# Transposes of the identity in the planned stands of TensorE, in a block of attention between two expert layers

## Chip, core and metric

The kernel runs on one core of a Trainium2 chip. Time is the device time of one execution in microseconds (us); lower is better. The five engines are TensorE (PE, its weight loads shown apart as PEld), VectorE (DVE), ScalarE (ACT), GpSimd (POOL) and SyncE (SP); each works through its own queue of instructions in order.

## What is computed

The input is x, 2 sequences of 4,096 tokens of width 256, in float32. The reference, cut to its steps:

```python
x = x + 0.5 * ffn(layernorm(x), gate_w, w1, w2, w3)
x = x + attn(layernorm(x), Wq, Wk, Wv, Wb, conv_q_w, conv_k_w, conv_v_w, rms_w, Wo)
x = x + 0.5 * ffn(layernorm(x), gate_w, w1, w2, w3)
```

`ffn` sends each token to 2 of 8 experts by a softmax over `x @ gate_w`; an expert is `(silu(xs @ w1) * (xs @ w3)) @ w2` with 128 hidden columns. `attn` has 4 heads of 64 columns: projections, a causal convolution over 4 tokens and silu for q, k and v, then a recurrence over chunks of tokens with a 64 x 64 state per head (a triangular system per chunk, `mid = U - W S`, an output, and `S = S + mid.T @ K`), a root-mean-square norm and `Wo`.

## The kernel before

**Tiles and stages.** Work comes in units of 4 x 128 tokens (256 of each sequence). For an expert layer, units are taken in groups. `prepare` (line 739) normalises, routes and scatters the rows of a group into DRAM by expert (`slots`, POOL's indirect DMAs, line 712). `experts` (line 793) takes 256 slots at a time: two weight tiles `we` by DMA, the rows `xi` by DMA, four transposes into the PSUM tile `pxi`, a copy to `xiT`, eight products into `p13` (the profile's `p_a`, `p_b`; a product of float32 shows as two rows), silu and product into `hs`, two products into `py`, a copy to `yo` and a DMA to `made`. `combine` (line 852) gathers rows back (line 730) and adds.

Attention is done in steps of two units. `project` (line 884) makes q, k, v (`ptx`, `pj`, `pb`). `gram` and `substitute` (line 999) solve 32 x 32 triangles on VectorE through DRAM. For each chunk of 128 tokens `inverse` (line 1031) loads the results (`XT`, `X`) and builds the inverse from small products (`pp`, `px`, `pq`, `pz`), and `advance` (line 1081) runs the recurrence (`pa`, `pk`, `pv`, `pks`, `pmid`, `po`, `pds`); `finish` norms, transposes (`pto`) and projects (`pyo`).

**Names.** `_a` and `_b` in a tile's name stand for the first and the second expert layer (and `_a` for tiles of attention's units). PSUM tiles come from one pool with two buffers for each of four tags, `tr`, `fa`, `at` and `y`; each buffer is one bank.

**What sets the order.** Nearly no instruction is issued where it is written. `plan` (class `Plan`, line 43) records each call with its reads, writes and a cost; `order` (line 183) then plays the whole program once, before it is issued, as a greedy list schedule over the five engines, and `issue` (line 360) gives the operations out in that order. PE, DVE, ACT and SP then follow it as it stands. The model in `order`:

- `cost` (line 111) gives the time of a VectorE, ScalarE or GpSimd operation by its columns; `dma` (line 105) that of a transfer, which lands 1.4 us after its issue (2.0 us for an indirect one) and its own time.
- `stream` (line 144) gives the time and the weight of a product; a transpose of 128 columns takes 0.84 x 128 + 2 ns, 55 more behind a stand.
- TensorE's clock is modelled in windows of 3,413 ns: after a window that streamed fewer than 1,450 columns, everything takes 1.9 times as long in the next (line 335).
- A PSUM tile is given a buffer when the operation that first writes it has all its predecessors planned (`offer`, line 273); the operation starts no sooner than the buffer came free (line 285).

`t` is the planned start of the operation that is taken next, and `free["tensor"]` the planned end of TensorE's last one. Where `t` is later, the plan sees TensorE stand.

Of the kernel before, what the change touches and what calls it, by code (L numbers as in the profile page):

```python
# [42 lines left out]
class Plan:  # L43
# [11 lines left out]

    def __init__(self, nc):
        self.nc = nc
        self.ops, self.tiles = [], {}
        for name in self.ENGINES:
            setattr(self, name, Plan.Engine(self, name))  # L60

# [14 lines left out]
    class Pool:  # L76
# [5 lines left out]
        def tile(self, shape, dtype, tag=None, name=None, bufs=None):  # L82
            kw = {} if bufs is None else {"bufs": bufs}
            t = self.pool.tile(shape, dtype, tag=tag, name=name, **kw)
            self.plan.tiles[t.tensor.name] = (id(self), tag, bufs or self.bufs)
            return t

    @staticmethod
# [94 lines left out]
    def order(self):  # L183
        ops, N = self.ops, len(self.ops)
# [67 lines left out]
        own, rank, count, slots = [[] for _ in range(N)], {}, {}, {}  # L252
        for m, (pool, tag, bufs) in self.tiles.items():
            if m in users:
                key = (pool, tag)
# [4 lines left out]
                    own[k].append(m)  # L260
        left = {m: len(users[m]) for m in rank}
        ended = {m: 0.0 for m in rank}
        given, taken, waiting = set(), dict.fromkeys(slots, 0), {}
        need = [len(b) for b in before]
        for k in range(N):
            for j in before[k]:
# [1 line left out]
        at = [0.0] * N  # L268
        coming = {e: [] for e in self.ENGINES}
        ready = {e: [] for e in self.ENGINES}  # L270
        free = dict.fromkeys(self.ENGINES, 0.0)

        def offer(k):
            new = sorted((m for m in own[k] if m not in given), key=lambda m: rank[m])
            want = {}
            for m in new:
                key = self.tiles[m][:2]
                n = want.get(key, 0)
                if rank[m] != taken[key] + n or len(slots[key]) <= n:
                    waiting.setdefault(key, []).append(k)  # L280
                    return
                want[key] = n + 1
            for m in new:
                key = self.tiles[m][:2]
                at[k] = max(at[k], heapq.heappop(slots[key]) + self.HEED[ops[k][0]])
                taken[key] += 1
                given.add(m)
            heapq.heappush(coming[ops[k][0]], (at[k], k))
            for key in want:
                for j in waiting.pop(key, ()):  # L290
                    offer(j)

        for k in range(N):
            if need[k] == 0:
                offer(k)
# [3 lines left out]

        W, window, streamed, pace = 3413.0, 0, 0.0, 1.9  # L300
        last = (True, 128, 128, 128, 0)
        result = []
        while len(result) < N:
            best = None
            for e in self.ENGINES:
                while coming[e] and coming[e][0][0] <= free[e]:
                    k = heapq.heappop(coming[e])[1]
                    heapq.heappush(ready[e], k)
                if ready[e]:
                    t = free[e]  # L310
                elif coming[e]:
                    t = coming[e][0][0]
                else:
                    continue
                if best is None or t < best[0]:
                    best = (t, e)
            t, e = best
            while coming[e] and coming[e][0][0] <= t:
                heapq.heappush(ready[e], heapq.heappop(coming[e])[1])
            k = heapq.heappop(ready[e])  # L320
            cost = ops[k][4]
            if cost[0] == "dma":
                _, size, soft, extra = cost
                lane = turn[soft] % self.QUEUES
                t = max(t + extra, lanes[soft][lane] + 50)
                end = moved = max(t + (2000 if soft else 1400), moved) + size
                lanes[soft][lane] = end
                turn[soft] += 1
                free[e] = t + (1278 if soft else 430)
            else:  # L330
                if e == "tensor":
                    end = t
                    for product in cost:
                        while end >= (window + 1) * W:
                            pace = 1.0 if streamed >= 1450 else 1.9
                            window, streamed = window + 1, 0.0
                        c, m = self.stream(product, last, end > free[e] + 6)
                        streamed, last = streamed + m, product
                        end = free[e] = end + c * pace
                    end += 165  # L340
                else:
                    end, free[e] = t + cost[1], t + cost[0]
            result.append(k)
            for j in behind[k]:
                need[j] -= 1
                same = ops[j][0] == e == "tensor"
                at[j] = max(at[j], free[e] if same else end + self.HEED[ops[j][0]])
                if need[j] == 0:
                    offer(j)
            for m in own[k]:  # L350
                left[m] -= 1
                ended[m] = max(ended[m], end)
                if left[m] == 0:
                    key = self.tiles[m][:2]
                    heapq.heappush(slots[key], ended[m])
                    for j in waiting.pop(key, ()):
                        offer(j)
        return result, max(free.values())

    def issue(self):  # L360
        order, _ = self.order()
        for k in order:
            self.ops[k][1]()


@with_exitstack
def kernel(
# [22 lines left out]
    E, _, FH = w1.shape  # L390
# [28 lines left out]
    plan = Plan(nc)  # L419
# [17 lines left out]
    ident = const.tile([P, P], F32, name="ident")  # L437
# [42 lines left out]


    nc = plan


    WROW = 2 * KC * FH + DM
# [30 lines left out]
    slots = [dram.tile([NTL * P, DM], F32, name=f"slots_{i}") for i in range(2)]  # L516
# [775 lines left out]
    for n in range(-1, NS):  # L1292
        (i0, f0), (i1, f1) = PLAN[n + 1], PLAN[n + 2]
        c0, c1 = cost_of(i0, f0), cost_of(i1, f1)
        for part in range(2):
# [11 lines left out]
            if n + 1 < NS:  # L1307
                c = PROJECT_COST + 2 * GRAM_COST + part * SUB_COST
# [56 lines left out]
```

## Time and profile before

| | |
|---|---|
| median of 10 executions | 2186.46 us (2176.47 to 2193.56) |
| profiled execution, time / span | 2173.45 us / 2171.6 us |
| mean granted clock of TensorE | 0.859 |
| PE busy | 1625.7 us, 12,324 rows |
| DVE, POOL, ACT busy | 1198.8, 732.4, 728.2 us |
| moved by DMA | 418.01 MB, a mean of 192 GB/s |

The span runs from the first to the last instruction. Busy time is the time in which an engine has an instruction in work. The profile cuts the span into 40 slices and gives the busy share of each in tenths; `PEclk` is the clock that TensorE was granted, in tenths of full speed. A line of waits names who waited for whom, the sum in us, how many times, and the longest. In a timeline, a line holds the start, the duration, engine, line (72 is the helper that issues all planned operations), operation, output and inputs, and how many; the bracket at its end is the idle time before it. In a table of stretches a line holds the stretch, its length, the busy time and count of each engine, the granted clock, the DMA engines' busy share and GB/s.

### The profile page before, as it was taken

What the parts mean: (1) busy time and instruction counts of PE and PEld (TensorE: products, weight loads), DVE (VectorE), ACT (ScalarE), POOL (GpSimd) and SP (SyncE); (2) the same over time, 40 slices, a digit from 0 to 9 for tenths busy, and PEclk for the clock granted to TensorE, in tenths of its full rate; (3) what the DMA queues carried; (4) which work ended last, traced back from release to release, by engine and by line L of the source; (5) the groups of instructions that cost most, each with busy time, mean ns of one, the idle gap of its engine ahead of it and who ended that gap; (6) DMA issues with size and microseconds to landing.
All of it is one profiled execution on the core that took longest, in us unless ns stands there. A gap on an engine that the chain in (4) does not pass through costs nothing. (4 is left out here: it accounts for less than half of the span.)

```text
span 2171.6 us, 36805 instructions
## 1 busy us (share of the span) xinstructions
PE 1625.7 (75%) x12324; PEld 1267.6 (58%) x12324; DVE 1198.8 (55%) x3737; ACT 728.2 (34%) x1402; POOL 732.4 (34%) x833
## 2 busy tenths in 40 slices
PE   2645965689849996995988599669989858797653
PEld 1434643467637775774766377557757646686442
DVE  4423733786467666466556846656684447344422
ACT  1232443233534432343432324523332432231220
POOL 3144145411664311114455111653110462024342
PEclk7778987989869996997979789869988879698777
DMA  9778776745577552546668234765453768368875
GB/s 370 240 260 276 241 227 209 236 117 159 160 227 213 162 164 62 145 121 191 208 189 260 83 98 119 249 198 158 119 152 105 234 216 265 109 206 278 266 259 152
DMA packets 369406, 418.01 MB, mean 192 GB/s; under 512 B 124480, under 2 KB 304704, under 8 KB 369216
## 3 DMA queue, kind: packets, MB, share of 16 engines
q1 hardware_dynamic: 343280, 345.35, 51.9%
q0 software_dynamic: 24576, 67.14, 9.3%
q10 hardware_dynamic: 1360, 3.16, 0.4%
q8 instruction: 98, 1.61, 0.3%
q14 instruction: 92, 0.75, 0.1%
HBM read 288.51 MB, written 130.15 MB: 193 GB/s over the span
## 5 line engine op out<-in xcount | busy, mean ns | idle before, releaser
L72 PE MATMUL p_b<-xiT_b,we_b 128*128 128x128 f32 x1344 | 210.6, 298 | 67.2 <-ACT hs_b L72 41.3
L72 PEld LDWEIGHTS p_b<-xiT_b,we_b 128*128 128x128 f32 x1344 | 182.5, 204 | 106.7 <-ACT hs_b L72 56.6
L72 PE MATMUL p_a<-xiT_a,we_a 128*128 128x128 f32 x1280 | 195.9, 292 | 49.3 <-ACT hs_a L72 37.4
L72 DVE SCALAR_TENSOR_TENSOR cv_a<-pre_a,cw_sb,cv_a 128x512 f32<-128x512 f32 x288 | 213.3, 746 | 27.6 <-ACT cv_a L72 24.2
L72 PEld LDWEIGHTS p_a<-xiT_a,we_a 128*128 128x128 f32 x1280 | 169.2, 198 | 86.0 <-ACT hs_a L72 52.5
L72 PE MATMUL pj_a<-xT_a,wp_sb 128*128 128x512 f32 x384 | 195.8, 621 | 10.7 <-ACT cv_a L72 9.2
L712 POOL DMA_INDIRECT slots<-row_b,sli_b x128 | 129.6, 1013 | 154.8 <-ACT row_b L72 71.4
L712 POOL DMA_INDIRECT slots<-row_a,sli_a x128 | 129.5, 1012 | 144.7 <-ACT row_a L72 62.5
L730 POOL DMA_INDIRECT got_b<-made,sli_b x128 | 126.7, 989 | 143.9 <-DMA made<-yo_b 38.5
L730 POOL DMA_INDIRECT got_a<-made,sli_a x128 | 127.6, 997 | 109.2 <-DVE x_a_2c L72 19.8
L72 POOL TENSOR_TENSOR rr<-ms,mhalf 128x8 f32<-128x8 f32 x32 | 53.7, 1679 | 270.8 <-DVE ms L72 236.8
L72 PE MATMUL pxi_a<-ident,xi_a 128*128 128x128 f32 x320 | 53.7, 289 | 72.4 <-DMA xi_a<-slots 72.0
L72 POOL COPY carry<-pre_a 128x6 f32<-128x6 f32 x96 | 27.9, 291 | 229.0 <-ACT pre_a L72 228.6
L72 PE MATMUL py_a<-we_a,hs_a 128*128 128x256 f32 x320 | 93.0, 408 | 9.2 <-DVE hs_a L72 6.3
L72 DVE TENSOR_TENSOR hs_b<-p_b,hs_b 128x256 f32<-128x256 f32 x84 | 35.6, 423 | 115.1 <-PE p_b L72 110.4
L72 PE MATMUL py_b<-we_b,hs_b 128*128 128x256 f32 x336 | 96.2, 405 | 3.7 <-DVE hs_b L72 1.5
L72 PEld LDWEIGHTS pj_a<-xT_a,wp_sb 128*128 128x128 f32 x384 | 67.9, 198 | 52.3 <-issue 32.8
L72 ACT COPY pre_a<-pj_a 128x512 f32<-128x512 f32 x96 | 56.2, 585 | 121.3 <-PE pj_a L72 109.2
L72 DVE TENSOR_TENSOR hs_a<-p_a,hs_a 128x256 f32<-128x256 f32 x80 | 33.9, 423 | 111.6 <-PE p_a L72 106.4
L72 PEld LDWEIGHTS pxi_a<-ident,xi_a 128*128 128x128 f32 x320 | 41.0, 149 | 91.8 <-DMA xi_a<-slots 68.2
L72 PE MATMUL pxi_b<-ident,xi_b 128*128 128x128 f32 x336 | 55.9, 293 | 46.3 <-DMA xi_b<-slots 46.3
L72 PE MATMUL pyo<-wo_sb,oT 128*128 128x256 f32 x256 | 71.9, 426 | 20.0 <-ACT oT L72 20.0
(240 smaller groups left out, 3658.3 us busy)
## 6 DMA issues: line engine op xcount, KB each, us to landing
we_b<-wcat SPq DMA_DIRECT2D x168, 384.0 KB
we_a<-wcat SPq DMA_DIRECT2D x160, 384.0 KB
xi_b<-slots SPq DMA_DIRECT2D x84, 256.0 KB
made<-yo_b SPq DMA_DIRECT2D x84, 256.0 KB
xi_a<-slots SPq DMA_DIRECT2D x80, 256.0 KB
made<-yo_a SPq DMA_DIRECT2D x80, 256.0 KB
slots<-XT SPq DMA_DIRECT2D x9, 1024.0 KB
x_a<-in_L_attn_x_dram SPq DMA_DIRECT2D x32, 256.0 KB
```

Of the source, the lines that this page charges most:

```text
L72: self.plan.add(self.name, lambda: real(*args, **kw), ins, outs, cost)
L712: ins = tc.nc.gpsimd.indirect_dma_start(out=dst, out_offset=bass.IndirectOffsetOnAxis(ap=slot, axis=0), in_=row, in_offset=None,)
L730: return tc.nc.gpsimd.indirect_dma_start(out=got, out_offset=None, in_=src, in_offset=bass.IndirectOffsetOnAxis(ap=slot, axis=0),)
```

## The change

Each PSUM tile with 128 partitions and at least 128 columns is kept by name with a view of its first 128 columns (`banks`). When `offer` gives such a tile its buffer, it also enters the tile in `blank` with the time from which the buffer is free; when an operation that writes the tile is planned, the tile leaves `blank`.

When TensorE's next operation is taken, the planner looks at the time between the end of its last operation and the start `t`. As long as some tile is blank, it takes the one that has been free longest and puts a transpose of the identity (`filler`: 128 x 128) into it, as long as that transpose ends before `t - 100 - 0.1 * gap` ns by the plan. The tile's name goes into the order, and `issue` gives out the transpose there. The model counts it as a product like any other, for TensorE's time and for the clock. The operation that the tile is meant for writes over it later. The diff:

```diff
--- before.py
+++ after.py
@@ -55,7 +55,7 @@
 
     def __init__(self, nc):
         self.nc = nc
-        self.ops, self.tiles = [], {}
+        self.ops, self.tiles, self.banks = [], {}, {}
         for name in self.ENGINES:
             setattr(self, name, Plan.Engine(self, name))
 
@@ -83,6 +83,11 @@
             kw = {} if bufs is None else {"bufs": bufs}
             t = self.pool.tile(shape, dtype, tag=tag, name=name, **kw)
             self.plan.tiles[t.tensor.name] = (id(self), tag, bufs or self.bufs)
+            if t.space == bass.MemoryType.PSUM:
+                axes = " ".join("abc"[: len(shape) - 1])
+                flat = t.rearrange(f"p {axes} -> p ({axes})") if len(shape) > 2 else t
+                if shape[0] == 128 and flat.shape[1] >= 128:
+                    self.plan.banks[t.tensor.name] = flat[:, 0:128]
             return t
 
     @staticmethod
@@ -260,7 +265,7 @@
                     own[k].append(m)
         left = {m: len(users[m]) for m in rank}
         ended = {m: 0.0 for m in rank}
-        given, taken, waiting = set(), dict.fromkeys(slots, 0), {}
+        given, taken, waiting, blank = set(), dict.fromkeys(slots, 0), {}, {}
         need = [len(b) for b in before]
         for k in range(N):
             for j in before[k]:
@@ -282,9 +287,12 @@
                 want[key] = n + 1
             for m in new:
                 key = self.tiles[m][:2]
-                at[k] = max(at[k], heapq.heappop(slots[key]) + self.HEED[ops[k][0]])
+                since = heapq.heappop(slots[key]) + self.HEED[ops[k][0]]
+                at[k] = max(at[k], since)
                 taken[key] += 1
                 given.add(m)
+                if m in self.banks:
+                    blank[m] = since
             heapq.heappush(coming[ops[k][0]], (at[k], k))
             for key in want:
                 for j in waiting.pop(key, ()):
@@ -299,8 +307,10 @@
 
         W, window, streamed, pace = 3413.0, 0, 0.0, 1.9
         last = (True, 128, 128, 128, 0)
-        result = []
-        while len(result) < N:
+        filler = (True, 128, 128, 128, 0)
+        result, done = [], 0
+        while done < N:
+            done += 1
             best = None
             for e in self.ENGINES:
                 while coming[e] and coming[e][0][0] <= free[e]:
@@ -319,6 +329,21 @@
                 heapq.heappush(ready[e], heapq.heappop(coming[e])[1])
             k = heapq.heappop(ready[e])
             cost = ops[k][4]
+            gap = t - free[e]
+            while e == "tensor" and blank:
+
+                m = min(blank, key=lambda m: blank[m])
+                f = max(free[e], blank[m])
+                while f >= (window + 1) * W:
+                    pace = 1.0 if streamed >= 1450 else 1.9
+                    window, streamed = window + 1, 0.0
+                c, n = self.stream(filler, last, f > free[e] + 6)
+                if f + c * pace > t - 100 - 0.1 * gap:
+                    break
+                streamed, last, free[e] = streamed + n, filler, f + c * pace
+                result.append(m)
+            for m, _ in ops[k][3]:
+                blank.pop(m, None)
             if cost[0] == "dma":
                 _, size, soft, extra = cost
                 lane = turn[soft] % self.QUEUES
@@ -360,7 +385,10 @@
     def issue(self):
         order, _ = self.order()
         for k in order:
-            self.ops[k][1]()
+            if k in self.banks:
+                self.nc.tensor.transpose(self.banks[k], self.filler, self.filler)
+            else:
+                self.ops[k][1]()
 
 
 @with_exitstack
@@ -480,6 +508,7 @@
 
 
     nc = plan
+    plan.filler = ident
 
 
     WROW = 2 * KC * FH + DM
```

## Prediction

> **What bounds the kernel now.** I read the page's busy shares and slices first. Its chain of waits names only some 5% of the span, all from the last 120 us, so I put it aside and went to the slices, PE's waits, the stretches at half clock and the timeline.
>
> ```profile
> PE 1625.7 (75%) x12324; PEld 1267.6 (58%) x12324; DVE 1198.8 (55%) x3737; ACT 728.2 (34%) x1402; POOL 732.4 (34%) x833
> ...
> PE   2645965689849996995988599669989858797653
> ...
> PEclk7778987989869996997979789869988879698777
> ```
>
> TensorE (PE) is the busiest engine and stands for 2171.6 - 1625.7 = 545.9 us. In many slices PE is at 8 or 9, in others it waits, and the granted clock dips in the slices where it waits. The table of busy time in stretches, asked for every stretch whose granted clock is one half, gives 32 of them; the five longest in attention, and the sum:
>
> ```profile
> 830.94:865.07 34.13, 21.05 (x208) 0.50 0.22 52
> ...
> 1216.64:1264.43 47.79, 27.02 (x222) 0.50 0.15 37
> ...
> 1400.96:1448.75 47.79, 19.97 (x168) 0.50 0.64 193
> ...
> 1616.00:1639.90 23.90, 20.69 (x205) 0.50 0.17 30
> ...
> 1851.52:1882.24 30.72, 23.00 (x215) 0.50 0.28 64
> ...
> sum 613.60, PE 282.89; mean PE 8.84
> ```
>
> PE does 282.9 us of its work at half clock. In the five stretches a long wait for XT is followed by a nearly unbroken run of products, with DMA at 0.15 to 0.28 in four of them: there PE itself is the limit. What half clock costs is seen by the same products at both. At half:
>
> ```profile
> 854.10 3.67 PE L72 MATMUL pmid<-r,XT 128*128 128x64 f32 x16
> ...
> 863.45 1.89 PE L72 MATMUL pds<-mid,kt 128*128 128x128 f32 x8
> ```
>
> and at full:
>
> ```profile
> 464.38 2.00 PE L72 MATMUL pmid<-r,XT 128*128 128x64 f32 x16
> ...
> 469.58 1.11 PE L72 MATMUL pds<-mid,kt 128*128 128x128 f32 x8
> ```
>
> From the start of pmid to the end of pds is 11.24 us at half, 6.31 us at full. The waits of PE say where the stands are:
>
> ```profile
> PE pp L72 <- DMA XT<-XTd: 78.1, 12, 27.9
> PE pxi_a L72 <- DMA xi_a<-slots: 72.0, 5, 34.3
> PE pxi_b L72 <- DMA xi_b<-slots: 46.3, 3, 23.4
> PE p_b L72 <- ACT hs_b L72: 41.3, 76, 2.3
> ```
>
> There are few long stands, for transfers (with we and X, 228.2 us of the 545.9), and many short ones for ScalarE and VectorE (0.54 us each for hs_b).
>
> **Does a transpose raise the clock?** The clock changes at the ends of stretches of 3.41 us. Two of these in a row, at half clock, and the one behind them:
>
> ```profile
> 2025.61:2029.02 3.41, 2.95 (x4) 1.00 (x4) 1.03 (x2) 0.55 (x1) 2.46 (x3) 0.50 0.78 197
> 2029.02:2032.43 3.41, 3.41 (x15) 2.40 (x13) 1.00 (x2) 1.54 (x3) 0.00 (x0) 0.50 0.61 210
> 2032.43:2035.85 3.42, 3.22 (x20) 2.73 (x20) 2.69 (x14) 1.52 (x4) 0.00 (x0) 1.00 0.62 181
> ```
>
> The timeline puts the products plt_b (4 rows of 512 columns, 2026.21 to 2030.11) across the first two. By time, 72% of the 2,048 columns, about 1,475, fall in the first, which did not raise the clock. The second holds the other 573, about 140 of py_b, and 8 transposes of 128 columns (1,024): some 1,740, and the clock rose. Without its transposes it has about 710, half of what did not suffice. So transposes count as products do, and some 1,500 to 1,700 columns in a stretch are enough. The same eight transposes at half and at full clock:
>
> ```profile
> 2029.91 1.91 PE L72 MATMUL pxi_b<-ident,xi_b 128*128 128x128 f32 x8
> ...
> 2034.61 1.04 PE L72 MATMUL pxi_b<-ident,xi_b 128*128 128x128 f32 x8
> ```
>
> That is some 0.21 and 0.11 us each behind the first: 16 per stretch (2,050 columns) at half, 31 at full. A filled stand raises the clock after one or two stretches and holds it. The Trainium skill, in "TensorE: Matmul & The Clock Gate", Part 4 (PE-mode transpose), speaks against the change: the full clock does not engage for transposes, since they do not count as busy time. By that rule nothing is gained, and the sum below would be its last term alone, a loss; the stretch above says otherwise, and I go by it.
>
> **The change, part by part.** It removes nothing.
>
> *Transposes in the stands.* After a stand of g the rule leaves 0.1 g + 0.1 us. Laid over PE's traced stands (0.11 us each, 0.055 more for the first of a stand) it fits 292 stands and at most 3,546 transposes, 406 us. The plan's stands are not the chip's, so this only sets the size. It adds as many weight loads, beside the transposes, and about 7,100 instructions to 24,648; the queues that carry instructions moved 2.4 MB of 418, so I cost their fetch at nothing.
>
> *Gain 1, the five attention stretches.* From pmid to pds each saves 11.24 - 6.31 = 4.93, and pa before it 2.19 - 1.16 = 1.03 (timeline, 16 products each): 6.0. I count nothing for pp, px, pq and pz ahead of them: small products in 10 us, which may let the clock fall again until pa. PE is unbroken, so this lies on the path. Between nothing and 5 x 6.0 = 30, I take four of five: **24 us**.
>
> *Gain 2, the rest of the half-clock work.* 282.9 - 111.7 (the five) = 171.2 us; at 1.04/1.91 it would take 93, so 78 us at most. Behind stands for xi the path is a chain through PE, ScalarE, VectorE and DMA, and half of the cold work may be beside it; and part of the stands will be filled too little to be warm at their end (next paragraph but one). A third: **26 us**, ends 0 and 78.
>
> *Loss, transposes where the chip has no stand.* A transpose too many delays whatever PE has behind it, in program order: all later products, and the hs, xiT, mid and yo of ScalarE and VectorE that wait for them. How good is the plan's clock? For 512-column work its formulas give 744 ns on VectorE and 588 on ScalarE, and the rows have 746 and 585; POOL's power 1,644 against 1,679; one scatter after another 1.28 against 1.27 us in the timeline. But it lands a scatter after 2.5 us, where the page has 3.7 to 4.2, and a we after some 2.5, where the chain of waits holds single waits of 4.9 and 5.7 for one. So stands for transfers are mostly longer than planned: no transpose is late there, but the clock may have fallen before work resumes. The risk is the other 545.9 - 228.2 = 318 us: 406 x 318/546 = 236 us of filling, in short stands behind two engines whose order can shift. Nothing in this trace shows the mismatch: bounds 0 and half, 118. The durations agree within some 2%, so I take a value near the low end, a tenth: **24 us**.
>
> *Moved waits.* A transpose now waits for the last reader of its bank, a ScalarE or VectorE copy, at the head of PE's queue. Where the plan has that reader early, products behind wait too; it is inside the loss. The planner also runs on with a warmer clock, so the orders of all five queues change; no row prices that, its sign is open, and I leave it at nothing.
>
> **Sum**: 24 + 26 - 24 = 26 us less. The profiled execution took 2173.45 us (span 2171.6 and 1.85 around it), so 2147. That execution is faster than all ten shown; their median is 13.0 above it: **2160 us**.
>
> **Rivals.** All times on the median's scale.
>
> *The planned stands are not the chip's (slower).* Place: short stands of the expert and projection phases, where PE is at 9 in the slices. Price: half of 236, 118 us, against gains of 50: 2254. It decides from 50/236, about a fifth, of that filling. For it: 75% busy and 406 more leave PE little room to catch up. Against it: the formulas agree with the rows. The milder form, in which the fillers don't warm what matters and the loss of 24 is all there is, gives 2210. Together 0.35.
>
> *Nearly all of it is kept (much faster).* 30 + two thirds of 78 (52) less 5: 2109. For it: the four stretches with DMA under 0.3. Against: PE's waits for DMA are planned short. 0.14.
>
> *Nothing to be seen.* The long stands hang on POOL's scatters and on transfers (POOL waits for rows, DMA at 0.5 to 1.0 in the stretches around xi), which a faster PE doesn't hasten, and gain and loss cancel: 2186. 0.10.
>
> The forecast, from 0.3% to about 2.5% less, has 0.41. A measurement of this kernel can tell some 0.3% (6.5 us) from no change: faster 0.55, within 0.10, slower 0.35. For 8 in 10 the range runs from 2095, a little below the much faster case, to 2250, into the slower one.
>
> **What would show it.** Right: rows of transposes out of ident alone into many tiles' banks; mean clock up from 0.859 to 0.92 or more; half-clock stretches down from 613.6 us to below 400; pmid's 16 products at 2.0 us in at least four of the five stretches; PE busy at 1,850 or more. Loss right: ScalarE's and VectorE's waits for p_b and p_a (130.0, 110.4, 95.6, 106.4 us) not up by more than a tenth. Wrong: clock unchanged under filled stands (transposes do not count); the clock at 0.95 and the span no shorter (half-clock work was beside the path); those waits up by a quarter or more (over-filled); or pp still waiting at half clock behind its long stands, which would mean stands planned far too short.

## The result, and the profile after

The changed kernel takes 2195.81 us (median of 15 runs, 2184.98 to 2205.87). The kernel before, run beside it, takes 2181.33 us (52 runs, 2164.1 to 2203.42). The ratio is 1.0066, with a 95% interval of 1.0047 to 1.0085: about 14 us slower. The forecast was 2160 us, faster; the time lies within the range given, and the sign is wrong.

The page of the changed kernel, its busy times and its slices:

```profile
PE 1940.3 (89%) x15522; PEld 1597.4 (73%) x15522; DVE 1196.0 (55%) x3737; ACT 724.9 (33%) x1402; POOL 734.2 (34%) x833
...
PE   9998998889989999998988899789989888988793
...
PEclk9999999989999998998999889889989899799997
```

PE has 3,198 more products in the records, the transposes, all of one line (L389), and is busy 314.6 us more. The dips of the clock are nearly gone: its mean is 0.938 where it was 0.859. In the table of all stretches at half clock (stretch, PE's busy time, clock) the sum is now:

```profile
sum 270.47, PE 215.94; mean PE 9.39
```

613.6 us at half clock have become 270.5. Without the transposes, PE's own products took 1586.2 us where they took 1625.7, and 198.3 us of them ran at half clock where 282.9 had. So PE spent 39 us less on its own work. The span of the profiled execution, 2188.2 us, is 17 us longer all the same.

PE's waits by what ended them:

```profile
PE p_b L72 <- ACT hs_b L72: 42.2, 77, 3.2
...
PE pxi_a L72 <- DMA xi_a<-slots: 12.1, 2, 7.0
PE pp L72 <- DMA XT<-XTd: 9.8, 9, 3.2
PE pxi_b L72 <- DMA xi_b<-slots: 6.8, 3, 4.0
```

The wait of 78.1 us for XT is now 9.8, and 12.1 and 6.8 us stand where 72.0 and 46.3 stood for xi. The stands were filled as the change says: PE stands 247.9 us in all, where it stood 545.9. The many short waits for hs_b have not moved (42.2 us, before 41.3).

The half clock that is left lies where the gain was to come from. The timeline of PE in the longest of the five attention stretches (start, duration, operation, tiles, count; the bracket is the idle time ahead of it):

```profile
1222.29 19.70 PE L389 MATMUL pp<-ident 128*128 128x128 f32 x179
1245.17 0.24 PE L72 MATMUL pp<-XT,L 32*32 32x32 f32 x2 [3.17 <-DMA XT<-XTd]
...
1251.07 1.93 PE L72 MATMUL pq<-XT,L 64*64 64x64 f32 x16 [1.41 <-issue]
...
1258.43 3.67 PE L72 MATMUL pmid<-r,XT 128*128 128x64 f32 x16
```

Here 179 transposes run at full clock, 0.11 us each. Then PE stands 3.17 us, the tenth that the rule leaves and what the transfer took longer than planned; then come pp, px, pq and pz, products of 32 and 64 columns; and pmid takes 3.67 us, the price at half clock. The table of stretches over the same place:

```profile
1242.00:1245.20 3.20, 0.03 (x1) 1.00 0.36 58
1245.20:1248.60 3.40, 2.24 (x59) 0.52 0.44 68
1248.60:1252.00 3.40, 1.99 (x39) 0.50 0.06 10
```

The stretch in which PE stands is still granted full clock, and the ones behind it half. In all five stretches that were to be warm, pmid takes 3.67 us as before (a table further down has them).

### The profile page after: what moved, and what is told of

The parts are those of the page before. It is cut to its first block, busy times and chain, and to the rows that moved or that the text cites. A ratio compares the mean times of both kernels' runs of the same rounds, so it can differ in the third digit from the quotient of the medians.

```text
span 2188.2 us, 43213 instructions
## 1 busy us (share of the span) xinstructions
PE 1940.3 (89%) x15522; PEld 1597.4 (73%) x15522; DVE 1196.0 (55%) x3737; ACT 724.9 (33%) x1402; POOL 734.2 (34%) x833
## 5 line engine op out<-in xcount | busy, mean ns | idle before, releaser
L72 PE MATMUL p_b<-xiT_b,we_b 128*128 128x128 f32 x1344 | 201.0, 290 | 65.9 <-ACT hs_b L72 42.2
L72 PEld LDWEIGHTS p_b<-xiT_b,we_b 128*128 128x128 f32 x1344 | 173.6, 196 | 99.7 <-ACT hs_b L72 57.1
L72 PE MATMUL pj_a<-xT_a,wp_sb 128*128 128x512 f32 x384 | 189.8, 608 | 9.8 <-ACT cv_a L72 6.1
L389 PE MATMUL pxi_a<-ident 128*128 128x128 f32 x1279 | 142.3, 273 | 0.0
L389 PEld LDWEIGHTS pxi_a<-ident 128*128 128x128 f32 x1279 | 140.2, 140 | 1.4 <-issue 1.1
L72 DVE TENSOR_TENSOR hs_b<-p_b,hs_b 128x256 f32<-128x256 f32 x84 | 35.6, 424 | 119.4 <-PE p_b L72 118.9
L72 DVE TENSOR_TENSOR hs_a<-p_a,hs_a 128x256 f32<-128x256 f32 x80 | 33.9, 424 | 117.8 <-PE p_a L72 109.8
L72 DVE TENSOR_TENSOR z<-lb,yb 128x31 f32<-128x31 f32 (+15 forms) x248 | 84.2, 340 | 4.0
L72 DVE TENSOR_TENSOR yb<-yb,z 128x31 f32<-128x31 f32 (+15 forms) x248 | 84.2, 339 | 3.7
```

Of the source, the lines that this page charges most:

```text
L72: self.plan.add(self.name, lambda: real(*args, **kw), ins, outs, cost)
L389: self.nc.tensor.transpose(self.banks[k], self.filler, self.filler)
```

## The experiments

A chunk is the work from pp to pds on 128 tokens of each sequence: there are 32, four to a step, and the five of the prediction are each the first of a step. A run's name stands in brackets behind its heading, and the quoted text is what was expected before it ran. A ratio is to the kernel before on the same chip, with its 95% interval; the quotient of two medians can differ from it by some tenths of a per cent. Diffs are against the changed kernel where nothing else is said; for a run in the order of before, the lines of fill_only that keep that order are in it too and are not shown again.

**The order alone** (order_only). The planner fills and orders as in the changed kernel, and no transpose is issued.

```diff
-            if k in self.banks:
-                self.nc.tensor.transpose(self.banks[k], self.filler, self.filler)
-            else:
+            if k not in self.banks:
                 self.ops[k][1]()
```

> The changed plan's order, with none of its transposes issued: it leaves out the fillers alone. Over-filling theory (the transposes delay PE where the chip has no stand): without them the loss of 0.66% goes, 0.995 to 1.002 of before. Order theory (the new order of the five queues costs, the transposes do not): 1.004 to 1.010.

Measured: 1.0045 [1.0014, 1.0076]. The changed order of the five queues costs some 10 us by itself (3 to 17).

**The transposes alone, in the order of before** (fill_only). They are placed with a copy of TensorE's time and of the clock's model, so that the plan goes on as if there were none.

```diff
-            while e == "tensor" and blank:
+            at_pe, state = free["tensor"], (window, streamed, pace, last)
+            while e == "tensor" and blank:
...
-                f = max(free[e], blank[m])
+                f = max(at_pe, blank[m])
...
-                streamed, last, free[e] = streamed + n, filler, f + c * pace
+                streamed, last, at_pe = streamed + n, filler, f + c * pace
                 result.append(m)
+            window, streamed, pace, last = state
```

> The order of before in all five queues, with transposes put into the stands that this plan sees (some 2,900), the plan itself not told of them. Over-filling theory: as slow as the change or slower, 1.003 to 1.012. Order theory: the warmer clock shows, 0.985 to 0.998.

Measured: 1.0039 [1.0011, 1.0067], with 2,895 transposes; half-clock products fell from 282.9 to 224.5 us. So the transposes lose by themselves, too, some 8 us. The two parts add up to 1.0084, and the whole has 1.0066 [1.0047, 1.0085].

**Long stands alone, short stands alone** (fill_long, fill_short). The kernel of the transposes alone, with one more condition:

```diff
-            while e == "tensor" and blank:
+            while e == "tensor" and blank and gap > 5000:
```

> As fill_only, but only in planned stands of over 5 us (some 2,290 transposes). Over-filling of short stands, as the prediction had it: nothing is late in long stands, and work behind them is warm, 0.988 to 0.998. Over-filling of stands for transfers, which the change's timeline shows at 199 to 225 us: 1.002 to 1.010. The clock buys nothing on the path: 0.998 to 1.002.

Measured: 1.0006 [0.9975, 1.0038], 2,290 transposes in 18 runs.

```diff
-            while e == "tensor" and blank:
+            while e == "tensor" and blank and gap <= 5000:
```

> As fill_only, but only in planned stands of up to 5 us (some 605 transposes, 70 us). Over-filling of short stands: 1.003 to 1.010. Over-filling of long stands: 0.997 to 1.002.

Measured: 1.0027 [0.9997, 1.0058], 605 transposes. Neither can be told from no change alone. The long stands hold four fifths of the transposes and give nothing.

**Only the stands for weights** (fill_we). The same kernel; transposes only ahead of the first expert products (tiles named p13, p_a and p_b in the trace).

```diff
-            while e == "tensor" and blank:
+            while e == "tensor" and blank and ops[k][3][0][0].startswith("p13"):
```

> Before's order, transposes only in the planned stands ahead of the expert products p_a and p_b (some 220, 24 us), which the plan sees for the weights. In fill_short all but a few runs of them end with no stand behind them. If these stands are not the chip's and PE is the limit there: 1.003 to 1.010, most of fill_short's loss. If the delay is taken up by later stands: 0.998 to 1.002.

Measured: 1.0067 [1.0038, 1.0096], some 15 us for 237 transposes in 33 runs; 27 of the runs end with no stand behind them. The same place in the timeline of the kernel before, and then of this one:

```profile
210.04 0.60 PE L72 MATMUL pxi_a<-ident,xi_a 128*128 128x128 f32 x4
211.20 0.94 PE L72 MATMUL p_a<-xiT_a,we_a 128*128 128x128 f32 x6 [0.55 <-DMA we_a<-wcat]
```

```profile
214.04 0.60 PE L72 MATMUL pxi_a<-ident,xi_a 128*128 128x128 f32 x4
214.47 3.55 PE L391 MATMUL p_a<-ident 128*128 128x128 f32 x31
217.86 0.83 PE L72 MATMUL p_a<-xiT_a,we_a 128*128 128x128 f32 x6
```

The plan has TensorE wait some 4 us for weights where the chip waits 0.55. The 31 transposes fill the planned stand, and p_a starts 3.2 us after pxi_a where it started 0.56 after. fill_short holds these runs and has 1.0027, on another chip; the intervals meet between 1.0038 and 1.0058, so the loss is some 8 to 13 us if both hold. The 237 transposes take 31.6 us of PE's time. That the loss is the sum of delays like this one is likely; only the delays are seen, not which of them reach the end.

**Does any other order cost as much?** (order_pace, order_heed) Two orders made for no purpose, without transposes, against the kernel before: one pace of the clock's model, and the time that the plan adds when TensorE frees a buffer.

```diff
-                            pace = 1.0 if streamed >= 1450 else 1.9
+                            pace = 1.0 if streamed >= 1450 else 1.85
```

> The kernel before with one number of the plan's clock changed (half clock taken as 1.85 times as slow, not 1.9): another order of some thousand rows, no transposes. It asks what any other order costs. If the change's order is bad because it was planned for a warm PE: within 0.998 to 1.002 here. If an order next to the one of before is by itself some tenths of a per cent off: outside of that.

Measured: 1.0077 [1.0044, 1.0110].

```diff
-    HEED = {"tensor": 54, "vector": 35, "scalar": 36, "gpsimd": 75, "sync": 60}
+    HEED = {"tensor": 60, "vector": 35, "scalar": 36, "gpsimd": 75, "sync": 60}
```

> The same question with another number: TensorE's delay in heeding a semaphore planned as 60 ns, not 54. No transposes. Within 0.998 to 1.002 if an order next to that of before is as good; outside if orders differ by tenths of a per cent by chance.

Measured: 1.0118 [1.0081, 1.0155]. Orders planned with one constant changed by a trifle cost 0.8 and 1.2%. So the 1.0045 of the changed order needs no reason of its own; why the order of before is the better one is not shown.

**The five attention stretches, held warm** (hold_pp, hold_more). In the order of before, only stands of over 2 us ahead of pp are filled, up to the planned end, and 8 transposes more are put ahead of px, pq and pz of such a chunk.

```diff
+            name, _, part = ops[k][3][0][0].partition("_")
+            part = "_".join(part.split("_")[:2])
+            pp = e == "tensor" and name == "pp"
+            if pp and gap > 2000:
+                hot.add(part)
...
-            while e == "tensor" and blank:
+            while e == "tensor" and blank and pp and gap > 2000:
...
-                if f + c * pace > t - 100 - 0.1 * gap:
+                if f + c * pace > t - 0 - 0.0 * gap:
...
+            if e == "tensor" and name in ("px", "pq", "pz") and part in hot:
+                result += [ops[k][3][0][0]] * 8
```

> Before's order. Transposes only in planned stands of over 2 us ahead of pp, to their planned end, and in those six chunks 8 more ahead of each of px, pq and pz, into their own banks, so that the small products' stretches of 3.41 us are full enough for the clock. If the clock of the attention stretches is on the path (Gain 1 of the prediction, which the change did not get since the clock fell among the small products): pmid's 16 products at 2.0 us instead of 3.67 and 0.985 to 0.995. If a faster PE there only waits for something else: the same 2.0 us for pmid, and 0.998 to 1.005.

Measured: 1.0003 [0.9974, 1.0032]. As the table below shows, two of the five chunks became 7 to 8 us shorter, a third was warm only from pmid on and gained nothing, and two stayed at half clock and became longer, by 3.5 and 1.5 us. In sum the five are 10.0 us shorter in this trace, and the time is the same within 6 or 7 us: what the chunks gain need not all reach the end. A second try closes the stand (0.9 us beyond the planned end) and adds more:

```diff
-                if f + c * pace > t - 100 - 0.1 * gap:
+                if f + c * pace > t + 900 - 0.0 * gap:
...
+        HOLD = {"px": 12, "pq": 11, "pz": 8}
...
+            if e == "tensor" and name in HOLD and part in hot:
+                result += [ops[k][3][0][0]] * HOLD[name]
```

> As hold_pp, with the transposes ahead of pp running 0.9 us past the planned end of the stand, and 12, 11 and 8 ahead of px, pq and pz in place of 8, 8, 8. In hold_pp the clock held in two of the five cold chunks (pp to the end of pds 16.7 and 18.0 us in place of 24.7) and fell in two (28.0 and 26.1). If too few columns in the stretch that holds pp is why: pmid at 2.0 us in all, pp to pds at 17 to 20 us, and 0.985 to 0.995. If a warm chunk is only followed by a longer wait: the same pmid and 0.998 to 1.004.

Measured: 0.9868 [0.9829, 0.9908], 2154.46 us against 2179.36 (25 us by these medians, 29 by the ratio), with 933 transposes where the change has 3,198. By the ratios this version is faster than both kernels. The chunk shown above, in its timeline:

```profile
1216.99 20.12 PE L399 MATMUL pp<-ident 128*128 128x128 f32 x173
1237.04 0.69 PE L72 MATMUL pp<-XT,L 32*32 32x32 f32 x32
1238.19 1.53 PE L399 MATMUL px<-ident 128*128 128x128 f32 x12 [0.46 <-ACT pm L72]
...
1241.78 1.39 PE L399 MATMUL pq<-ident 128*128 128x128 f32 x11 [1.03 <-DVE XT L72]
...
1244.18 1.09 PE L399 MATMUL pz<-ident 128*128 128x128 f32 x8
...
1248.20 2.00 PE L72 MATMUL pmid<-r,XT 128*128 128x64 f32 x16
```

No stand is left ahead of pp, 31 transposes lie among the small products, and pmid takes 2.00 us. From the start of pp to the end of pds, in us, with the time of pmid's 16 products in brackets, for the five chunks of the prediction:

| kernel | 1st | 2nd | 3rd | 4th | 5th |
|---|---|---|---|---|---|
| before | 24.56 (3.67) | 24.73 (3.67) | 25.82 (3.67) | 24.75 (3.67) | 24.59 (3.67) |
| changed | 23.84 (3.67) | 24.42 (3.67) | 24.75 (3.67) | 24.84 (3.67) | 23.20 (3.67) |
| hold_pp | 28.02 (3.67) | 16.68 (2.00) | 25.62 (2.00) | 18.02 (2.00) | 26.08 (3.67) |
| hold_more | 17.44 (2.00) | 17.45 (2.00) | 24.32 (3.34) | 18.61 (2.00) | 17.50 (2.00) |

Four chunks that become 6.1 to 7.3 us shorter make 27.6 us; the ratio makes 29 us (0.0132 x 2179; 20 to 37 by its interval). That these agree so closely is in part chance: the two profiled executions behind the rows, one of each kernel, are only 15 us apart. The same kernel on another chip (hold_more_b):

> hold_more once more, to see whether its gain stands on a second chip: 0.983 to 0.991 if it does; 0.995 to 1.005 if the first was the chip's or chance.

Measured: 0.9906 [0.9871, 0.9941], some 21 us. The gain stands on both chips.

**The other long stands** (fill_rest). In the order of before, only stands planned at over 5 us, behind the first 100 us, not those ahead of pp.

```diff
-            while e == "tensor" and blank:
+            while e == "tensor" and blank and gap > 5000 and t > 100e3 and not ops[k][3][0][0].startswith("pp_"):
```

> Before's order, transposes only in planned stands of over 5 us that are neither in the first 100 us nor ahead of pp: ten runs, some 1,240 transposes, mostly ahead of pxi. Few of them can be late (a stand of 1 to 7 us was left behind nearly all of them in fill_long). If warm work behind these stands is on the path: 0.992 to 0.997 (up to 3 us for each). If the clock has fallen again by the time the work resumes, or POOL and DMA set the pace: 0.998 to 1.002.

Measured: 1.0014 [0.9984, 1.0043], with 1,237 transposes. They ran at full clock but for some 5 us, and the work behind them did not:

```profile
142.95 33.46 PE L391 MATMUL pxi_a<-ident 128*128 128x128 f32 x305
178.76 1.54 PE L72 MATMUL pxi_a<-ident,xi_a 128*128 128x128 f32 x6 [2.35 <-DMA xi_a<-slots]
180.55 2.50 PE L72 MATMUL p_a<-xiT_a,we_a 128*128 128x128 f32 x10 [0.25 <-ACT xiT_a L72]
...
186.73 1.28 PE L72 MATMUL p_a<-xiT_a,we_a 128*128 128x128 f32 x10
```

The same ten products take 2.50 us behind a stand of 2.35 us, and 1.28 us some 6 us later. In the 10 us behind the ten runs of transposes, the clock is at half for 1.8 to 6.8 us behind eight of them. Half-clock products are 275.1 us, before 282.9.

**The first 100 us** (fill_setup). In the order of before, only stands that end in the plan's first 100 us.

```diff
-            while e == "tensor" and blank:
+            while e == "tensor" and blank and t < 100e3:
```

> Before's order, transposes only in the first 100 us: some 500, of which a run of 317 is put between the two halves of one unit's transposes ptx, which before the change followed one another at once. If that run delays the second half and all behind it: 1.001 to 1.003 (3 to 6 us). If routing waits for something else: 0.999 to 1.001.

Measured: 1.0024 [1.0001, 1.0046] for 497 transposes. This filling gives nothing, and costs some 5 us if anything.

**The other long stands up to their end** (rest_full, hold_rest). As fill_rest, without the tenth, and without the stands ahead of pg.

```diff
-                if f + c * pace > t - 100 - 0.1 * gap:
+                if f + c * pace > t - 0 - 0.0 * gap:
```

> As fill_rest without the run ahead of pg, and filled to the planned end of the stand, nothing left. If the clock's fall in the tenth that is left is why fill_rest gained nothing: less half clock in the 10 us behind the runs, and 0.992 to 0.998. If that work is not on the path, or what a warm start gives is lost where the chip's stand is shorter than planned (by some 1.5 us at the first, from fill_rest's rows): 0.999 to 1.004 with the warmer clock.

Measured: 1.0201 [1.0165, 1.0237], on a chip on which the kernel before takes 2220.27. With hold_more beside it in one kernel:

> hold_more and rest_full in one. If both gains are real and in different places: their product, 0.980 to 0.985. If only the attention chunks are on the path: 0.986 to 0.991, as hold_more.

Measured: 1.0081 [1.0050, 1.0113]. A new thing was seen in both traces: transposes that stood still, one by one, waiting for nothing that the profile shows. The first run of 340 took 62.6 us in rest_full, where 0.11 us each makes 37. Counted where one transpose starts over 0.3 us behind the last, less the 0.11 that it takes, these standstills come to 63.9 and 48.6 us. To tell whether the kernel or the chip makes them, rest_full was run twice more (rest_full_b, rest_full_c), each time beside a kernel that had shown none (hold_more, and fill_rest as fill_rest_c):

> rest_full once more. If the standstills came with that chip: none here, and as fill_rest or a little faster, 0.995 to 1.003. If they come with runs of over some 190 transposes while POOL scatters: again some 60 us of them and 1.015 to 1.025 on any chip.

Measured: 1.0205 [1.0165, 1.0245], with 54.6 us of standstills; hold_more_b, on the same chip, has none between its transposes.

> fill_rest again. If the chip decides: on a chip with before near 2217 us, standstills and 1.010 to 1.020; with before near 2180 us none and 0.998 to 1.004. If the length decides: no standstill on either, 0.998 to 1.004.

Measured: 1.0142 [1.0091, 1.0194]. This is fill_rest, unchanged, on a chip on which the kernel before takes 2208.14 us: 36.4 us of standstills where it had none. The same run of transposes as shown above:

```profile
142.08 21.38 PE L391 MATMUL pxi_a<-ident 128*128 128x128 f32 x192
164.34 0.38 PE L391 MATMUL pxi_a<-ident 128*128 128x128 f32 x2 [0.87 <-issue]
...
179.34 1.17 PE L391 MATMUL pxi_a<-ident 128*128 128x128 f32 x3 [1.55 <-issue]
...
194.74 0.82 PE L72 MATMUL pxi_a<-ident,xi_a 128*128 128x128 f32 x6
```

> rest_full again, on the same chip. If the chip decides: with before near 2180 us no standstill, and the question of its first submission is answered, 0.992 to 1.004; with before near 2217 us, 1.015 to 1.025. If the length decides: 1.015 to 1.025 on either.

Measured: 1.0192 [1.0149, 1.0235], with 48.7 us of standstills.

The kernel before itself, on that chip (before_c):

> The kernel before, for its profile on that chip: near 2180 us with rows as in the first profile if the chip is like the first ones; near 2217 us if it is like the last two, and then longer in the stretches where the others stood still, if those come from the chip.

One run: 2205.13 us. PE's idle time ended by "issue" (gaps over 0.3 us) is 33.1 us here, where the first profile of the kernel before has 11.8. But 15.7 of the 33.1 lie ahead of p_a and p_b, where the first profile has waits for hs instead (78.7 us there, 71.1 here). So fill_rest stands still on one chip and not on another; whether the kernel before meets the same thing is not shown. rest_full never ran on a chip without standstills, and what a warm clock behind the xi stands is worth was not measured.

## Why the prediction was wrong, point by point

The steps that failed are the two gains: the clock rose in the stands, and had fallen again when the work that was to pay for it began. To this comes a term that was put at nothing, the changed orders. Of the signs named for "right", the transposes in the banks, the mean clock (0.938), the half-clock stretches (270.5 us) and PE's busy time (1940.3 us) all came; only pmid's duration told that nothing was won.

*A transpose raises the clock: right.* The rule of the Trainium skill that was weighed against it ("TensorE: Matmul & The Clock Gate", Part 4) does not hold for these transposes in float32: in fill_rest, 305 of them with nothing else took 33.46 us, with the clock granted in full all the while.

*Gain 1, the five attention stretches: failed; forecast 24 us.* In the trace the five chunks together are 3.4 us shorter. The step that failed is "which may let the clock fall again until pa", in which I saw the danger, gave it no price, and took four of five as warm. In the changed kernel pmid is at 3.67 us in five of five.

That PE is busy does not keep the clock: between 1252.0 and 1255.4 it is busy 3.34 of 3.40 us, and the clock stays at half. Nor do bare columns. By time some 1,700 stream in that stretch, most of them through 64 x 64 of the array, where 1,536 of 128-row products and transposes raised the clock in the kernel before (421.34 to 424.75: two rows of plt_a and four transposes). So the small products count for less than their columns, and the 1,500 to 1,700 of the prediction hold for wide products; the kernel's plan, in `stream`, counts a 64 x 64 product at a quarter of a wide one, by which the stretch has some 620.

hold_more fills its stands ahead of pp past their planned end and puts 31 transposes among the small products; with these four of five chunks are warm, and the kernel is 25 to 29 us shorter than the one before. So the work is on the path, and the size was about right (24 to 30); the filling had to reach on into the small products. hold_pp, with fewer and without the 0.9 us, warmed fewer; how the two edits share in it was not tried. Two readings behind this term were loose: the five are not the longest stretches at half clock while attention runs (984.54 to 1015.26 and 1721.82 to 1762.78 have 30.72 and 40.96 us, with experts' work among it), though they hold the most products, and the wait for XT ahead of the fourth and the fifth was only 2.3 and 4.4 us.

*Gain 2, the rest: not got; forecast 26 us.* The prediction had "part of the stands will be filled too little to be warm at their end" and took a third all the same. fill_rest, which fills the stands for xi and the others of over 5 us, gains nothing, and its trace shows the work behind eight of ten runs at half clock for a time: the tenth of a long stand, and a transfer that lands later than planned, are time enough for the clock to fall. The Trainium skill, in "TensorE: Matmul & The Clock Gate", "Why this matters for your kernels", asks for no gap in TensorE's work over some 3 us. Here less was enough: behind the run of 305 transposes the clock fell 2.06 us into a stand of 2.35 us (at 178.47). In another place of fill_rest it fell at 1018.15, behind a stretch with 1.36 us of products between a stand of 1.40 us and one of 3.26 that was 1.07 us old (PE busy, clock):

```profile
1015.20:1018.60 3.40, 1.36 (x7) 0.93 1.00 342
1018.60:1022.00 3.40, 1.67 (x4) 0.50 0.79 191
```

Whether the work behind xi stands would shorten the span if it were warm stays open.

*Loss: the size came about right by luck, the place was wrong; forecast 24 us.* It was a tenth of the filling put into "short stands behind two engines whose order can shift", and of stands for transfers it said "no transpose is late there". fill_we shows the opposite: in the place shown a stand for weights is planned at some 4 us and is 0.55, and filling such stands costs 15 us (8 to 21 by its interval, 8 to 13 if fill_short holds as well). The prediction had read 4.9 and 5.7 us for single transfers of weights in the chain of waits and taken from them that PE stands longer for weights than planned. PE's own waits for weights in the kernel before are about 1 us each (sum, times, longest):

```profile
PE p_b L72 <- DMA we_b<-wcat: 20.1, 17, 3.4
PE p_a L72 <- DMA we_a<-wcat: 11.0, 13, 2.6
```

The sign that was named for over-filling, the waits for hs up by a quarter, was a bad one: they are 132.5, 118.9, 92.2 and 109.8 us, none up by more than 8%, and the loss is there.

*Changed orders at nothing: failed.* order_only costs 10 us (3 to 17), as much as the whole effect but for 4 us. Two other small shifts cost 17 and 26. The prediction left the sign open; the order of before is a good one, and three of three tried beside it are worse, so a loss was the likelier of the two.

*The sum with measured terms*: 0 + 0 - 15 - 10 = 25 us slower, or 18 to 23 with 8 to 13 for the weights, where 14 were measured. The single terms carry some 7 us each way, so that the difference can be that, or a gain of the clock that no experiment isolates. fill_only and order_only make 18, which is inside the interval. The case nearest to the result in its mechanism is the milder form of the slower rival, in which the fillers don't warm what matters and the loss is all there is; it was given 2210 us.

## What to carry to other kernels

Ask of each filled wait whether the clock is still high where the work that pays begins: look at a product's time there (here pmid, 3.67 or 2.00 us), since the mean clock can rise (0.859 to 0.938) and the half-clock time fall by more than half (613.6 to 270.5 us) while the span gets longer. Fill up to the work and among its small products, only where the work behind is bound by TensorE, and only stands that the trace shows, not those that a plan computes. This kernel, whose order was found by a planner, lost some tenths of a per cent to a per cent by each of three new orders; so test the order alone and the operation alone.

## What the runs showed of the hardware that was not expected

On three chips (the kernel before at 2208, 2217 and 2220 us) long runs of transposes stood still in steps of mostly 0.7 to 3.5 us, 36 to 64 us in an execution, while GpSimd's scatters and gathers ran; on the chip with 2179 fill_rest had none, and on the one with 2208 it had. A long run beside such transfers is not enough: in hold_more_b, on one of the three chips, a run of 264 transposes lies beside 15 of them and does not stand still. The packets of the queues that carry instructions look alike with and without the standstills (a median of about 0.9 us); which resource it is stays open.

The clock can fall in a stand of only 2.35 us, and stays at half for 6.83 us. Small products on a part of the array did not raise it in a stretch in which they kept PE busy for 3.34 of 3.40 us. And three orders of the same work, two of them made by shifting one constant of the plan by 3 and by 11%, differ from the first by 0.45, 0.77 and 1.18%.
